# Two-bank tiles for the score maxima and for gate and up, three banks for everything else, in a two-layer transformer kernel

## The chip, the cores and the metric

The kernel runs on one core of a Trainium2 chip. The metric is the device time of one execution in microseconds (us), median of several runs. A core has a matrix engine (TensorE, PE in the profile, with its weight loads PEld), a vector engine (VectorE, DVE), an activation engine (ScalarE, ACT), GpSimd (POOL) and SyncE (SP), which issues DMAs. TensorE writes its results into PSUM, which this kernel divides into eight banks of 512 float32 elements in each of 128 partitions; VectorE and ScalarE read them from there.

## What is computed

Two transformer layers on x of 2 x 1024 x 256 float32 values. In each layer attention and a feed-forward network both start from the layer norm of x and are added to x. The change touches layer 0:

```python
xn = _layernorm(x, axis=-1)
x = x + _L0_attn_ref(xn, ...) + _L0_ffn_ref(xn, ...)

# _L0_attn_ref: 32 query heads, 8 key and value heads, 8 values a head, rope, causal
scores = jnp.einsum('bhqd,bhkd->bhqk', q, k_rep) / scale
scores = jnp.where((kpos > qpos)[None, None], -jnp.inf, scores)
attn = jax.nn.softmax(scores, axis=-1)
out = jnp.einsum('bhqk,bhkd->bhqd', attn, v_rep)
return out.transpose(0, 2, 1, 3).reshape(B, T, C) @ Wo + bo

# _L0_ffn_ref: 256 -> 1024 -> 256, operands rounded to e4m3, results in bfloat16
ff_gate = _qdot(x, w_gating[0])
gate_value = jax.nn.gelu(ff_gate)
ff1 = _qdot(x, w_gating[1])
outputs = _qdot(gate_value * ff1, w_linear)
```

Layer 1 has its own attention and a feed-forward network with ternary weights.

## The kernel before

Layer 0's attention (`attention0`) handles one block of 128 queries after another: `order` is the blocks (batch, i) of batch 0 rising and of batch 1 falling. A block i sees (i + 1) x 128 keys. Two passes are made over its scores.

The first finds the row maxima. A **unit** (`max_unit`) computes the scores of one, two or four pairs of heads into two banks, e = 0 and 1, which come from the two halves of the array's rows: `nc.tensor.matmul` at L843 for each e, the causal mask added by matmuls at L824 (`add_mask`). Then VectorE reduces each bank with its own `tensor_reduce` at L855. There are 304 units and 608 reductions. When a block's units are done, `take_max` (L869 to L873) splits the maxima into three bfloat16 parts, and `turn_max` transposes them and sends them through DRAM into the rows of the queries that subtract the maximum.

The second pass is made of 288 **weigh steps** (`weigh`). A step opens with two matmuls at L907 into two banks (e = 0, then e = 1), adds two more onto them, adds a mask (L824) on the diagonal, and ScalarE takes the exponential of each bank (L919). Every second step is preceded by a **gather** (L927): it multiplies the exponentials of two earlier steps with the values into the bank `acc`. Around it `normalise` (ot, L942), `turn_rows` (at, L958) and `output` (ao, L966) bring a finished group of heads out.

Between two weigh steps `one_slot` puts other work on TensorE: first one or several units of maxima of a later block, as a running credit of their cost allows, then a **piece** of the feed-forward network. In the pieces of `ffn0`, gate and up of 128 hidden columns for 512 tokens are two matmuls each (L284); ScalarE evicts each with a copy (L287), then GELU and rounding follow on ScalarE and VectorE in further pieces, and `out_piece` (f0o, L244) multiplies with the second weight. Other users of banks in this stage are the transposes of the layer norm (lnt, L178), the values (vp, L790), the maxima's transpose (mt, L878) and the group sums of layer 1's ternary weights (tps, L328).

TensorE's instructions run in the order in which the program makes them (`manual_schedule`). On the other engines the framework orders them, with `tc.issue_after(reduced.ins)` putting VectorE's share of a piece behind the last reduction made. A tile of a pool waits until a bank of that pool is free. The eight banks are divided so:

```python
ps_s = es.enter_context(tc.tile_pool(name="a0s", bufs=3, space=PSUM))
ps_t = es.enter_context(tc.tile_pool(name="a0t", bufs=4, space=PSUM))
ps_acc = es.enter_context(tc.tile_pool(name="a0acc", bufs=1, space=PSUM))
```

`ps_s` serves the maxima and the projections of queries and keys (`project`), one bank for each tile; `ps_t` serves weigh steps, gate and up, and all the other users named above.

Of the kernel before, what the change touches and what calls it, by code (L numbers as in the profile page):

```python
# [10 lines left out]
F32 = mybir.dt.float32  # L11
BF = mybir.dt.bfloat16
# [36 lines left out]
def two_layers(ctx: ExitStack, tc: tile.TileContext, a: dict, out: bass.AP):  # L49
# [179 lines left out]
                load(m)  # L229
            yield  # L230

    def ffn0(pool, psp, weights, add_done):

        wg, wl = weights
        acts = {}

        def e_tile(dt, name):
            t = pool.tile([P, 1024], F32, tag="fe", name=name, bufs=1)
            return t if dt == F32 else t.bitcast(BF)[:, 0:1024]

        def out_piece(n, i):
            po = psp.tile([P, D], F32, tag="t", name=f"f0o{n}_{i}")
            for hc in range(NHC):
                nc.tensor.matmul(  # L244
                    po,
                    acts[n][hc // 2][:, hc % 2 * 512 + i * P : hc % 2 * 512 + (i + 1) * P],
                    wl[:, hc, :],
                    start=(hc == 0),
                    stop=(hc == NHC - 1),
                )  # L250
            ob = pool.tile([P, D], BF, tag="ob", name=f"ob{n}_{i}", bufs=1)
            nc.scalar.copy(ob, po)  # L252
            x_i = xs[4 * n + i]
            nc.gpsimd.tensor_tensor(x_i, x_i, ob, ALU.add)
            nc.gpsimd.tensor_scalar(ob, ob, 0.0, None, ALU.mult)
            nc.gpsimd.tensor_tensor(x_i, x_i, ob, ALU.add)
            nc.gpsimd.tensor_tensor(x_i, x_i, bo_bc, ALU.add)
            add_done(4 * n + i)

        order = (0, 1, 3, 2)  # L260
        for m, n in enumerate(order):
            wide = pool.tile([P, 1024], F32, tag="fs", name=f"fsx{n}", bufs=1)
            xq = pool.tile([P, 2, 512], BF, tag="xq", name=f"xq{n}", bufs=1)
            yield from e4m3(
                xq.rearrange("p k t -> p (k t)"),
                xnT[n].rearrange("p k t -> p (k t)"),
                e_tile(F32, f"fex{n}"),
                wide,
                False,
            )  # L270
            yield
            acts[n] = []
            for h2 in range(NHC // 2):
                nm = f"{n}_{h2}"
                wide = pool.tile([P, 1024], F32, tag="fs", name=f"fs{nm}", bufs=1)
                w1, f1 = (wide.bitcast(BF)[:, k * 1024 : (k + 1) * 1024] for k in range(2))
                g = pool.tile([P, 1024], BF, tag="fg", name=f"fg{nm}", bufs=1)
                w2 = pool.tile([P, 1024], BF, tag="fw", name=f"fw{nm}", bufs=1)
                for j in range(2):
                    hc = 2 * h2 + j  # L280
                    for u, to in enumerate((g, f1)):
                        ps = psp.tile([P, 512], F32, tag="t", name=f"gu{nm}_{j}{u}")
                        for k in range(2):
                            nc.tensor.matmul(  # L284
                                ps, wg[:, u, k, hc * P : (hc + 1) * P], xq[:, k, :], start=(k == 0), stop=(k == 1)
                            )
                        nc.scalar.copy(to[:, j * 512 : (j + 1) * 512], ps)  # L287
                    yield

                nc.scalar.activation(w1, g, AF.Square)  # L290
                nc.vector.tensor_mul(w1, w1, g)
                nc.vector.tensor_scalar(w1, w1, GELU_C1, None, ALU.mult)
                yield
                nc.vector.tensor_add(w1, g, w1)
# [384 lines left out]
    def attention0(w, qlast, tables):  # L679
# [11 lines left out]
        with ExitStack() as es:  # L691
            pool = es.enter_context(tc.tile_pool(name="a0", bufs=2))
            es.enter_context(tc.manual_schedule(engines={mybir.EngineType.PE}))
            dram = es.enter_context(tc.tile_pool(name="a0d", bufs=2, space=bass.MemoryType.DRAM))
            ps_s = es.enter_context(tc.tile_pool(name="a0s", bufs=3, space=PSUM))
            ps_t = es.enter_context(tc.tile_pool(name="a0t", bufs=4, space=PSUM))
            ps_acc = es.enter_context(tc.tile_pool(name="a0acc", bufs=1, space=PSUM))
            units = ternary_units(pool, ps_t)
            kst, vst, qst, scratch = {}, {}, {}, {}
# [13 lines left out]

            def project(weights, lo, width, bias, b, c, name):

                ps = [ps_s.tile([P, 512], F32, tag="s", name=f"{name}p{e}") for e in range(2)]
                for e in range(2):
                    for k in range(2):
                        nc.tensor.matmul(
                            ps[e],  # L720
                            weights[:, k, e * width + lo : e * width + lo + P],
                            xnT[2 * b + c][:, k, :],
                            start=(k == 0),
                            stop=(k == 1),
                        )
                cs = slice(c * 512, (c + 1) * 512)
                y = []
                for e in range(2):
                    t = pool.tile([P, 512], F32, tag=f"y{e}", name=f"{name}y{e}", bufs=1)
                    nc.vector.scalar_tensor_tensor(t, ps[e], bias[:, e : e + 1], rope[:, e, cs], ALU.add, ALU.mult)  # L730
                    y.append(t)

                engine = nc.gpsimd if b or c else nc.vector
# [98 lines left out]
            def max_unit(b, i, pairs, lo, width, part, masked):  # L832
                if (b, i) not in mx:
                    mx[b, i] = pool.tile([P, 2, 2, NH0 // 2], F32, tag="mx", name=f"mx{b}{i}", bufs=3)
                n = len(pairs)
                sc = [ps_s.tile([P, 512], F32, tag="s", name=f"m{b}{i}_{pairs[0]}_{part}{e}") for e in range(2)]
                four = masked and width == P
                if four:
                    add_mask([x.rearrange("p (h k) -> p h k", h=4) for x in sc], mask_q, True, False)
# [11 lines left out]
                        end = (s + 1) * width  # L851
                        add_mask([x[:, end - P : end] for x in sc], mask_q, False, True)
                nonlocal reduced
                for e in range(2):
                    reduced = nc.vector.tensor_reduce(  # L855
                        mx[b, i][:, part, e, pairs[0] : pairs[0] + n],
                        sc[e][:, : n * width].rearrange("p (s k) -> p s k", s=n),
                        AX.X,
                        ALU.max,
                        negate=True,  # L860
                    )

            def take_max(b, i):
                both = mx.pop((b, i))
# [204 lines left out]

            acc = ps_acc.tile([P, 512], F32, tag="acc", name="acc0")  # L1070
            nc.vector.memset(acc, 0.0)
            pieces = itertools.chain(conversions, ffn0(pool, ps_t, weights, add_done))
            at = 0
            credit = share = 0.0
            cost_left = sum(cost for _, cost, _ in maxima)
# [169 lines left out]
```

## Time and profile before

| | |
|---|---|
| median of 3 runs | 1220.97 us (1217.82 to 1224.71) |
| the profiled execution | 1217.11 us, span 1215.3 us |
| mean granted TensorE clock | 0.903 |
| busy, of the span | PE 1044.4 us, DVE 738.2, ACT 572.8, PEld 501.8, POOL 265.4 |
| reductions of maxima (L855) | 608, busy 373.3 us |
| exponentials (L919) | 576, busy 307.5 us |
| first and last weigh step (L907) | 88.8 and 795.8 us |

The span is the time from the first to the last instruction. Busy time of an engine counts overlapping instructions once. A row of a group gives its line in the kernel, the engine, the operation, the tiles written and read, its count, busy us and mean ns of one, and the idle time of the engine just before it with what ended that. A row of the timeline gives start and duration in us, consecutive instructions of one kind merged (x2), and in brackets the idle time before it. Matmuls overlap, and the ends shown for them are modelled: an engine shown busy may still have been held.

### The profile page before, as it was taken

The numbers are of one execution on the slowest core, as the hardware profiler recorded it, in microseconds if no ns is written. First come the engines' busy times: TensorE is split into PE (matmuls) and PEld (weight loads), VectorE is DVE, ScalarE is ACT, GpSimd is POOL, SyncE is SP. The second block draws the span as 40 slices with busy tenths as digits, with TensorE's granted clock in tenths as the row PEclk, the third lists the DMA queues.
The fourth block names the chain that finished last, engine by engine and source line by source line (L and its number), as shares of the span: only waits on it lengthen the run. The fifth ranks groups of instructions, "written<-read, shape, count | busy, mean of one in ns | idle before, by whom it ended". The sixth has DMA issues, their size and how long they took to land.

```text
span 1215.3 us, 19246 instructions
## 1 busy us (share of the span) xinstructions
PE 1044.4 (86%) x7467; PEld 501.8 (41%) x7484; DVE 738.2 (61%) x1416; ACT 572.8 (47%) x990; POOL 265.4 (22%) x277
## 2 busy tenths in 40 slices
PE   6464897896988989898989998989999999998884
PEld 3233332232332223232323333335676676675673
DVE  7576988886867898788895889253223223323220
ACT  1113353662645757575767775741424414414421
POOL 3021022104053010501014115234313212312100
PEclk9576897997898989997999999999999999999785
DMA  6721001103011010100010110038211421411202
GB/s 193 168 80 37 22 15 38 26 2 90 1 26 27 2 26 18 35 1 18 10 27 3 25 26 5 3 30 120 54 28 45 75 40 45 77 39 28 44 11 53
DMA packets 79012, 49.01 MB, mean 40 GB/s; under 512 B 31720, under 2 KB 73704, under 8 KB 78920
## 3 DMA queue, kind: packets, MB, share of 16 engines
q1 hardware_dynamic: 75960, 43.58, 16.7%
q0 software_dynamic: 2960, 4.20, 1.7%
q8 instruction: 59, 0.97, 0.3%
q14 instruction: 33, 0.27, 0.1%
HBM read 33.59 MB, written 15.73 MB: 41 GB/s over the span
## 4 chain that ended last, share of the span: by engine, by line
PE 57%; DVE 21%; DMA 7%; issue 4%; ACT 4%; POOL 3%; SPq 2%; ACTq 0%; POOLq 0%; DVEq 0%
DVE mx L855 12%; PE acc L927 9%; PE s L907 8%; PE f1gu L610 7%; PE f1o L641 5%; PE m L843 4%; PE sk L520 3%; PE sq L485 3%; PE gu L284 2%; PE m L824 2%; PE s L824 2%; PE ao L586 2%; ACT p L528 2%; DMA qkv<-all 2%; PE acc L535 1%
## 5 line engine op out<-in xcount | busy, mean ns | idle before, releaser
L855 DVE TENSOR_REDUCE mx<-m 128x1 f32<-128x512 f32 (+3 forms) x608 | 373.3, 656 | 114.5 <-PE m L843 66.9
L919 ACT ACTIVATE p<-s 128x512 f32<-128x512 f32 x576 | 307.5, 603 | 163.5 <-PE s L907 115.3
L927 PE MATMUL acc<-p,v 128*9 128x512 f32 x1152 | 165.5, 626 | 0.0
L843 PE MATMUL m<-k,qmain 64*128 64x512 bf16 (+3 forms) x384 | 94.7, 368 | 44.3 <-DVE mx L855 28.4
L610 PE MATMUL f1gu<-xnT,wgu 128*128 128x512 f32 x256 | 118.9, 609 | 0.0
L843 PE MATMUL m<-kmain,qmain 64*128 64x512 bf16 (+3 forms) x384 | 82.4, 335 | 19.9 <-DVE mx L855 18.1
L824 PEld LDWEIGHTS <-ident_h 64*128 64x128 bf16 x1088 | 60.4, 97 | 92.3 <-issue 53.6
L843 PEld LDWEIGHTS <-qmain 64*128 64x128 bf16 x768 | 50.1, 100 | 89.0 <-issue 63.3
L824 PE MATMUL m<-mask_q,ident_h 64*128 64x128 bf16 (+1 forms) x832 | 82.0, 239 | 3.8 <-DVE mx L855 2.8
L618 DVE TENSOR_TENSOR h<-f1gu,h 128x512 f32<-128x512 f32 x32 | 22.1, 692 | 100.4 <-PE f1gu L610 97.0
L907 PE MATMUL s<-qlast,k 35*128 35x512 bf16 x288 | 66.3, 405 | 14.5 <-DMA qlast<-mscr 14.5
L907 PE MATMUL s<-qmain,k 64*128 64x512 bf16 x288 | 68.8, 409 | 11.3 <-ACT ob L252 5.8
L970 POOL TENSOR_TENSOR x<-x,aos 128x256 f32<-128x256 f32 x16 | 12.7, 792 | 300.5 <-ACT aos L969 300.5
L622 POOL TENSOR_TENSOR sq<-h 128x512 f32<-128x512 f32 x28 | 29.1, 1039 | 189.7 <-DVE h L618 189.7
L907 PEld LDWEIGHTS <-k 64*128 64x128 bf16 (+1 forms) x576 | 22.2, 97 | 114.5 <-issue 106.7
L610 PEld LDWEIGHTS f1gu<-xnT,wgu 128*128 128x128 f32 x256 | 48.1, 197 | 49.4 <-issue 49.3
L907 PE MATMUL s<-qmain,kmain 64*128 64x512 bf16 x288 | 64.2, 391 | 4.2 <-ACT p L919 2.4
L493 DVE TENSOR_REDUCE m<-sq 128x16 f32<-128x2048 f32 x16 | 36.7, 2292 | 44.8 <-PE sq L485 43.2
L907 PE MATMUL s<-qlast,klast 35*128 35x512 bf16 x288 | 61.2, 387 | 0.0
L641 PE MATMUL f1o<-k,h 128*128 128x256 f32 x256 | 58.9, 387 | 0.0
L641 PEld LDWEIGHTS f1o<-k,h 128*128 128x128 f32 x256 | 49.1, 194 | 8.2 <-issue 1.3
L907 PEld LDWEIGHTS <-kmain 64*128 64x128 bf16 x288 | 15.0, 94 | 78.1 <-issue 73.9
(267 smaller groups left out, 1588.1 us busy)
## 6 DMA issues: line engine op xcount, KB each, us to landing
qmain<-qscr SPq DMA_DIRECT2D x64, 96.0 KB
qkv<-all SPq DMA_DIRECT2D x16, 384.0 KB
qscr<-ptq SPq DMA_DIRECT2D x32, 96.0 KB
x<-in_x SPq DMA_DIRECT2D x16, 128.0 KB
qmain<-qscr SPq DMA_DIRECT2D x32, 64.0 KB
qs<-qkv SPq DMA_DIRECT2D x16, 128.0 KB
ks<-qkv SPq DMA_DIRECT2D x16, 128.0 KB
vs<-qkv SPq DMA_DIRECT2D x16, 128.0 KB
```

The lines of the kernel that those rows point to most:

```text
L485: nc.tensor.matmul(ps[:, s, r, :], columns(q, slice(S * s, S * s + HD + 8), 4 * b + r), columns(k, slice(S * s, S * s + HD + 8), 4 * b + r ...
L493: nc.vector.tensor_reduce(m, ps, AX.X, ALU.max, negate=True)
L520: nc.tensor.matmul(ps[:, s, r, :], columns(k, slice(S * s, S * s + HD + 9), 4 * b + r), columns(q, slice(S * s, S * s + HD + 9), 4 * b + r ...
L610: nc.tensor.matmul(ps[g], wgu[:, k, g * HID + hc * P : g * HID + (hc + 1) * P], xnT[n][:, k, :], start=(k == 0), stop=(k == 1),)
L622: nc.gpsimd.tensor_tensor(sq, h, h, ALU.mult)
L641: nc.tensor.matmul(po, hs[hc // 2][:, hc % 2, i * P : (i + 1) * P], wp[:, hc, :], start=(hc == 0), stop=(hc == NHC - 1),)
L824: nc.tensor.matmul(out[e], ident_h[rows, t, :], rhs, start=start and t == 0, stop=stop and t == 1)
L843: nc.tensor.matmul(sc[e][:, s * width : (s + 1) * width], qst[b, i][0][rows, p, :], kst[b][0][rows, p // 4, lo : lo + width], start=not fo ...
L855: reduced = nc.vector.tensor_reduce(mx[b, i][:, part, e, pairs[0] : pairs[0] + n], sc[e][:, : n * width].rearrange("p (s k) -> p s k", s=n ...
L907: nc.tensor.matmul(sc[e], kst[b][n][rows, u, j * P : (j + 1) * P], qst[b, i][n][rows, 4 * u : 4 * u + 4, :], start=n == 0, stop=n == 1 and ...
L919: nc.scalar.activation(p, sc[e], AF.Exp, scale=scale)
L927: nc.tensor.matmul(acc[32 * s : 32 * s + HD0 + 1, :], vst[b][:, j, 4 * G + s, :], ps[s], start=(j == 0), stop=(j == i),)
```

## The change

The maxima and the projections take one tile of two banks in place of two tiles of one bank; two such tiles make up the pool. One `tensor_reduce` reads both banks of a unit. Gate and up of one hidden chunk go into one two-bank tile of the same pool, and one copy evicts both; for that gate and up stand side by side in one buffer (`gf`), and `w1` moves to the buffer that held the gate. The pool for everything else has three banks in place of four.

```diff
-    def ffn0(pool, psp, weights, add_done):
+    def ffn0(pool, psp, ps_pair, weights, add_done):
...
-                w1, f1 = (wide.bitcast(BF)[:, k * 1024 : (k + 1) * 1024] for k in range(2))
-                g = pool.tile([P, 1024], BF, tag="fg", name=f"fg{nm}", bufs=1)
+                gf = wide.bitcast(BF).rearrange("p (u t) -> p u t", u=2)
+                w1 = pool.tile([P, 1024], BF, tag="fg", name=f"fg{nm}", bufs=1)
+                g, f1 = gf[:, 0], gf[:, 1]
...
-                    for u, to in enumerate((g, f1)):
-                        ps = psp.tile([P, 512], F32, tag="t", name=f"gu{nm}_{j}{u}")
+                    ps = ps_pair.tile([P, 2, 512], F32, tag="s", name=f"gu{nm}_{j}")
+                    for u in range(2):
                         for k in range(2):
                             nc.tensor.matmul(
-                                ps, wg[:, u, k, hc * P : (hc + 1) * P], xq[:, k, :], start=(k == 0), stop=(k == 1)
+                                ps[:, u],
+                                wg[:, u, k, hc * P : (hc + 1) * P],
+                                xq[:, k, :],
+                                start=(k == 0),
+                                stop=(k == 1),
                             )
-                        nc.scalar.copy(to[:, j * 512 : (j + 1) * 512], ps)
+                    nc.scalar.copy(gf[:, :, j * 512 : (j + 1) * 512], ps)
                     yield
...
-            ps_s = es.enter_context(tc.tile_pool(name="a0s", bufs=3, space=PSUM))
-            ps_t = es.enter_context(tc.tile_pool(name="a0t", bufs=4, space=PSUM))
+            ps_s = es.enter_context(tc.tile_pool(name="a0s", bufs=2, space=PSUM))
+            ps_t = es.enter_context(tc.tile_pool(name="a0t", bufs=3, space=PSUM))
...
-                ps = [ps_s.tile([P, 512], F32, tag="s", name=f"{name}p{e}") for e in range(2)]
+                ps = ps_s.tile([P, 2, 512], F32, tag="s", name=f"{name}p")
...
-                sc = [ps_s.tile([P, 512], F32, tag="s", name=f"m{b}{i}_{pairs[0]}_{part}{e}") for e in range(2)]
+                pair = ps_s.tile([P, 2, 512], F32, tag="s", name=f"m{b}{i}_{pairs[0]}_{part}")
+                sc = [pair[:, e] for e in range(2)]
...
-                for e in range(2):
-                    reduced = nc.vector.tensor_reduce(
-                        mx[b, i][:, part, e, pairs[0] : pairs[0] + n],
-                        sc[e][:, : n * width].rearrange("p (s k) -> p s k", s=n),
-                        AX.X,
-                        ALU.max,
-                        negate=True,
-                    )
+                reduced = nc.vector.tensor_reduce(
+                    mx[b, i][:, part, :, pairs[0] : pairs[0] + n],
+                    pair[:, :, : n * width].rearrange("p e (s k) -> p e s k", s=n),
+                    AX.X,
+                    ALU.max,
+                    negate=True,
+                )
...
-            pieces = itertools.chain(conversions, ffn0(pool, ps_t, weights, add_done))
+            pieces = itertools.chain(conversions, ffn0(pool, ps_t, ps_s, weights, add_done))
```

More of the change, by code (lines that the diff above doesn't have):

```diff
@@ L719, in project @@
                         nc.tensor.matmul(
-                            ps[e],
+                            ps[:, e],
                             weights[:, k, e * width + lo : e * width + lo + P],
@@ L729, in project @@
                     t = pool.tile([P, 512], F32, tag=f"y{e}", name=f"{name}y{e}", bufs=1)
-                    nc.vector.scalar_tensor_tensor(t, ps[e], bias[:, e : e + 1], rope[:, e, cs], ALU.add, ALU.mult)
+                    nc.vector.scalar_tensor_tensor(t, ps[:, e], bias[:, e : e + 1], rope[:, e, cs], ALU.add, ALU.mult)
                     y.append(t)
```

## The prediction

> **What bounds the kernel now.** I read the busy time by windows first, then the chain of waits, the groups kept apart by shape, the list of waits, and last the timeline, row by row.
>
> ```profile
> PE 57%; DVE 21%; DMA 7%; issue 4%; ACT 4%; POOL 3%; SPq 2%; ACTq 0%; POOLq 0%; DVEq 0%
> ...
> 700.00:750.00 50.00, 47.14 (x457) 19.44 (x456) 43.63 (x95) 33.52 (x65) 14.28 (x14) 1.00 0.09 18
> ...
> L855 DVE TENSOR_REDUCE mx<-m 128x1 f32<-128x512 f32 x384 | 245.8, 684 | 68.4 <-PE m L843 47.3 <-PE m L824 20.9
> L855 DVE TENSOR_REDUCE mx<-m 128x1 f32<-128x384 f32 x128 | 65.7, 551 | 21.7 <-PE m L824 20.9
> L493 DVE TENSOR_REDUCE m<-sq 128x16 f32<-128x2048 f32 x16 | 36.7, 2292 | 44.8 <-PE sq L485 43.2 <-DMA out<-x 1.5
> ...
> PE m L843 <- DVE mx L855: 46.5, 84, 1.9
> ```
>
> Layer 0's attention lasts from 88.8 us, where the first weigh step begins, to 797. In a window there (us busy of 50: PE, PEld, DVE, ACT, POOL) no engine is full: PE has 47, DVE 44, ACT 34. PE runs a written order, so any wait in it is lost. The only large entry in the wait list that holds PE there is L843, the maxima's matmuls, waiting for the reduction at L855. The timeline shows how:
>
> ```profile
> 412.96 0.39 PE L907 MATMUL s<-qmain,k 64*128 64x512 bf16 x2
> 413.18 0.38 PE L907 MATMUL s<-qlast,k 35*128 35x512 bf16 x2
> 413.40 0.38 PE L843 MATMUL m<-k,qmain 64*128 64x512 bf16 x2
> 413.62 0.27 PE L824 MATMUL m<-mask_q,ident_h 64*128 64x128 bf16 x4
> 413.73 0.38 PE L907 MATMUL s<-qmain,k 64*128 64x512 bf16 x2
> 413.95 0.38 PE L907 MATMUL s<-qlast,k 35*128 35x512 bf16 x2
> 414.17 0.38 PE L843 MATMUL m<-k,qmain 64*128 64x512 bf16 x1
> 414.94 0.37 PE L843 MATMUL m<-k,qmain 64*128 64x512 bf16 x1 [0.40 <-DVE mx L855]
> 414.95 0.48 PE L824 MATMUL m<-mask_q,ident_h 64*128 64x128 bf16 x4
> 415.36 1.04 PE L927 MATMUL acc<-p,v 128*9 128x512 f32 x8
> ...
> 413.66 2.06 ACT L919 ACTIVATE p<-s 128x512 f32<-128x512 f32 x4 [0.74 <-PE s L907]
> 414.21 2.50 DVE L855 TENSOR_REDUCE mx<-m 128x1 f32<-128x512 f32 x4
> ```
>
> The columns are start, duration, engine, line. A weigh step (L907) opens at 412.96, a unit of maxima follows, a second step at 413.73, a second unit, a gather (L927). The two matmuls of a unit normally start 3 ns apart. At 414.17 and 414.94 they are 0.77 apart: with three single banks the second needs the bank that the previous unit's first reduction holds. The reported idle time (0.40) is less than the loss, since the first matmul is still shown running.
>
> So I measured the loss as the distance of the two starts, over all 384 pairs of L843: **102.4 us in 196 pairs** beyond 10 ns each. Of it 53.0 lies in 265 ordinary intervals from one weigh step to the next (at most two pairs of matmuls), 37.5 in 22 intervals with more (bursts), and 11.9 before 88.8 us.
>
> [...] 684 - 551 ns over 128 elements is 1.04 ns each, which leaves 151 ns fixed. [...] The change moves banks from one rotation to another.
>
> **The reduction.** 608 instructions become 304 of double width. L493 already reads four banks at 2292 ns, so two should take 1024 x 1.04 + 151 = 1.22 us. In runs back to back, records overlap: 2.50 us for four is 0.62 each, hence about 1.15 per double one. DVE saves 0.085 to 0.15 per pair, 26 to 46 us in all, of which only what holds PE counts. The first half can no longer start alone, but its two matmuls end nearly together, so I add nothing; if they don't, each unit is up to 0.2 later.
>
> **The maxima's banks.** With two pairs, a unit waits for the unit before last as a whole. That is at least one single reduction (0.6 us) earlier than now, so in ordinary intervals I let these waits go. In bursts DVE itself has no room (15 reductions in the 12.0 us from 428.4 to 440.4, DVE busy 93%); there only its saving counts. 126 reductions lie in bursts: 63 x 0.085 = 5.4 us, up to all 37.5 where DVE is not full. I take -9. Before 88.8 us the path goes through loads and POOL, DVE is 66% busy: -2, from 0 to -12.
>
> **Three banks for the rest.** This is the cost. A weigh step needs two banks, freed by the exponentials (L919) of the step before. With four banks it finds two free. With three, its second opening matmul must wait for the first exponential of the step before, and everything on PE behind it waits too. In the lines above: the step of 412.96 has its exponentials from 413.66, the first frees its bank at 413.66 + 0.60 (a single one), plus 0.05 until PE goes on, 414.31. The next step wants it at 413.73: **0.58 us late**. A step after a gather comes 1 us later and finds it free.
>
> I did this for every step: the end of the exponential plus 0.05, less the start of the matmul; with all other tiles of that pool (ot, at, ao, mt, tps, f0o, lnt, vp) in the rotation and gate/up taken out of it. The same rule with four banks, gate/up included, accounts to within 70 ns for 42 of the 58 steps whose second matmul is already late now, so I trust it. With three it makes 124 of 287 steps wait, 75.6 us. 110 of them are among the 144 steps that no gather precedes (65.2 us), 14 among the 143 others (10.4).
>
> These waits and the ones removed partly replace each other, so I went through the intervals in PE's order: subtract each distance removed, and where a bank is later than the shifted matmul, set the shift to it. In ordinary intervals this gives 83.8 us of lengthening and 44.4 of shortening: **+39.4**. Two things take from that. Twenty-three gathers already wait for exponentials now (10.5 us more than the usual length), as the last steps show:
>
> ```profile
> 776.21 2.07 ACT L919 ACTIVATE p<-s 128x512 f32<-128x512 f32 x4 [1.17 <-PE s L824]
> ...
> 776.48 1.89 PE L927 MATMUL acc<-p,v 128*9 128x512 f32 x8
> ```
>
> The gather takes 1.89 us where 1.04 is usual; a step that is late ahead of it only uses up this wait: -10 (0 to -10.5). And the exponentials of a late step are queued on ACT behind the earlier ones anyway, so the steps after gathers wait less than listed: half of 10.4, -5 (0 to -10).
>
> **Gate and up.** 32 evictions of 1024 elements replace 64 of 512 (609 and 593 ns). ACT's rows give 603 ns for 512 and 1877 for 2048, so 0.83 ns an element and 1.03 us for 1024: 0.17 x 32 = 5.4 us less of ACT, which is idle a third of the time there; I count 0 (0 to -5). Without that cover it would be the whole 5.4. In the maxima's rotation, gate and up now wait for the reduction of the unit before last: 18 of the 32 come earlier than that today, 5.1 us, and units behind them or behind one another 2.1. I take +4 (0 to +7). The exchange of w1 and g between two buffers leaves the instructions as they are; the buffer of f1 comes free earlier, that of the other is first written later: 0, within 1 us either way. No DMA and no step is moved, so SP's and POOL's queues keep their order; POOL waits for DVE in long idle stretches and gets nothing tighter.
>
> **Sum.** 39.4 - 10 - 5 - 9 - 2 + 4 = +17.4 us. The profiled execution took 1217.1 us (span 1215.3 and 1.8 around it); the median of the three runs is 3.9 above. So 1234.5 against the profile, and **1238** as a median. Layer 1, from about 800 us, is untouched and moves as a whole.
>
> **Rivals.**
> *Faster: ACT gives its bank back soon enough.* What speaks for it: 102 us of waits on DVE are at stake, and the rule applied to today's times ignores that a delayed PE meets a less loaded ACT. If bursts yield 20 and the early part 6, then 44.4 + 26 goes, and new waits of 40 come: -30, 1191. The deciding point: the waits at steps not behind a gather. The sum is zero when the whole of new waits, 69 net in my account, is 51, or 0.35 us for each of the 144 steps instead of 0.48. Against it: the 0.58 is a latency from PE to ACT and back, shown with ACT idle before it (0.74 in the row), which no slack shortens.
> *An even swap:* bursts yield 25 instead of 9: about +1, 1222.
> *Much slower:* a fixed rotation makes a step wait for the second exponential, 0.49 us later, where another bank is free. In a third of the 110 steps that is +18, with no help from the gathers +28 more at most: up to 1280. Against it: the few misfits of my rule with four banks.
> *The wide reduction isn't cheaper* (two banks at 2 x 684): the gain of bursts and of the early part goes, +11, 1249. L493 speaks against it.
>
> **How the numbers follow.** A measurement of this kernel can tell some 0.5% from no change, 6.1 us. My case 0.45, much slower and not cheaper 0.13 together, even swap 0.16, faster 0.26. The range reaches from half way into the faster rival to half way into the much slower one, 1206 to 1270. The unknown terms of my own case reach about as far. With bursts and early part at their best (-38.5) it is 1200. With all at their worst (gathers +10, steps after gathers +5, gate and up +3, bursts +3.6, early part +2) and the late half costing 0.1 us in each of 304 units (+30) it is 1292, and half way there 1265.
>
> **What would show it.** Reductions: 304, near 1.2 us each. The two matmuls of a unit start together outside bursts, and L843's waits on L855 fall from 46.5 us below 20. The second matmul of L907 starts late, some 0.5 us, in about 110 steps, most of them not behind a gather; PE's waits on L919 rise from 4.1 us to tens. Gate/up evictions: 32, near 1.03 us. Ordinary steps about 0.1 us longer, layer 1 as long as before. I am wrong if L907's pairs start together, if L843 still waits as much, or if the last weigh step ends before 795 us.

## The result, and the profile after

| | before | after |
|---|---|---|
| median (6 runs each) | 1217.33 us | 1229.42 us |
| lowest to highest | 1212.75 to 1224.71 | 1225.93 to 1230.88 |
| span of the profiled execution | 1215.3 us | 1229.1 us |
| first weigh step opens | 88.8 us | 85.5 us |
| last weigh step opens | 795.8 us | 808.9 us |

The changed kernel is slower: ratio 1.0085, 95% interval 1.0061 to 1.0108. The changed kernel's lines are numbered a little higher: the steps are L912, the maxima's matmuls L849, the reduction L860, the exponential L924. Its page sums the chain of waits so:

```profile
PE 56%; DVE 17%; ACT 10%; issue 5%; DMA 5%; POOL 4%; SPq 1%; ACTq 0%; POOLq 0%; DVEq 0%
```

The window from 700 to 750 us of the changed kernel (window and length, then busy us and count of PE, PEld, DVE, ACT and POOL, then the granted clock, the DMA's share and GB/s):

```profile
700.00:750.00 50.00, 44.06 (x421) 18.08 (x419) 39.22 (x64) 34.33 (x62) 11.38 (x10) 1.00 0.09 18
```

Its groups by shape (busy us and mean ns of one, then idle time ahead):

```profile
L860 DVE TENSOR_REDUCE mx<-m 128x2 f32<-128x1024 f32 x192 | 231.9, 1220 | 86.3 <-PE m L849 56.3 <-PE m L829 29.3
L860 DVE TENSOR_REDUCE mx<-m 128x2 f32<-128x768 f32 x64 | 60.1, 953 | 25.3 <-PE m L829 25.3
L292 ACT CAST fs<-gu 128x1024 bf16<-128x1024 f32 x32 | 32.4, 1012 | 37.3 <-PE gu L285 37.2
```

And its list of waits (sum in us, count, longest in us):

```profile
PE m L849 <- DVE mx L860: 33.7, 40, 2.3
PE s L912 <- ACT p L924: 31.4, 67, 3.2
```

The last of these rows read so in the kernel before:

```profile
PE s L907 <- ACT p L919: 4.1, 7, 1.5
```

Each new instruction takes what its rows foretold: 1220 ns for a reduction of two banks, 1012 ns for the eviction of gate and up. But in the chain DVE's share falls from 21 to 17% while ACT's rises from 4 to 10%, and PE is less busy in the same window, 44.06 us for 47.14. The steps' wait for ACT grew from 4.1 to 31.4 us. The timeline shows it in the cycle of two steps, two units and a gather, the same that the prediction took apart:

```profile
407.31 0.39 PE L912 MATMUL s<-qmain,k 64*128 64x512 bf16 x2
407.53 0.38 PE L912 MATMUL s<-qlast,k 35*128 35x512 bf16 x2
407.75 0.38 PE L849 MATMUL m<-k,qmain 64*128 64x512 bf16 x2
407.97 0.27 PE L829 MATMUL m<-mask_q,ident_h 64*128 64x128 bf16 x4
408.08 0.38 PE L912 MATMUL s<-qmain,k 64*128 64x512 bf16 x1
408.65 0.37 PE L912 MATMUL s<-qmain,k 64*128 64x512 bf16 x1 [0.20 <-ACT p L924]
408.66 0.58 PE L912 MATMUL s<-qlast,k 35*128 35x512 bf16 x2
408.89 0.58 PE L849 MATMUL m<-k,qmain 64*128 64x512 bf16 x2
409.11 0.47 PE L829 MATMUL m<-mask_q,ident_h 64*128 64x128 bf16 x4
409.51 1.04 PE L932 MATMUL acc<-p,v 128*9 128x512 f32 x8
410.48 0.39 PE L912 MATMUL s<-qmain,k 64*128 64x512 bf16 x2
```

The second unit's two matmuls (408.89) no longer wait for VectorE. Instead the second step's opening pair is torn apart, 408.08 and 408.65: 0.57 us, where 0.58 was foretold. The reported idle time is again smaller (0.20), because the first matmul is still shown running (0.38 us from 408.08). The torn opening also leaves a lag of 0.20 us between the two matmuls of the unit behind it, with no wait in their row. One wait has taken the place of the other: this cycle lasts 3.17 us where it took 3.38 before, and the next one 3.18 for 3.11.

The loss lies elsewhere. An interval is the time from one weigh step's opening to the next; an ordinary one has at most two pairs of the units' matmuls in it, a burst more. Call a pair torn when its two matmuls start over 50 ns apart. The 96 ordinary intervals in which a unit had been torn before come out 14.5 us shorter in sum, and the other 169 come out 36.6 us longer.

Counted over the whole trace as in the prediction, the distances between the starts of the two matmuls, where beyond 10 ns, are:

| us | before | after |
|---|---|---|
| two matmuls of a unit (L843, now L849) | 102.4 | 26.5 |
| two opening matmuls of a step (L907, now L912) | 30.3 | 72.7 |
| steps late by over 50 ns, without / with a gather ahead | 55 / 3 | 111 / 10 |

Of the 26.5 us, 22.6 lie behind torn openings and are for the most part the lag just described. These distances are a sign of where PE was held and no account of the time: their sum falls from 132.7 to 99.2 us, while the kernel gets slower.

Where the 13.8 us between the two profiled spans lie, interval by interval between the openings of the same steps: ordinary intervals +22.1 (66.3 longer, 44.2 shorter), bursts -5.7, up to the first step -3.3, after the last +0.6.

### The profile page after: what moved, and what is told of

The parts are those of the page before. It is cut to its first block, busy times and chain, and to the rows that moved or that the text cites. A ratio compares the mean times of both kernels' runs of the same rounds, so it can differ in the third digit from the quotient of the medians.

```text
span 1229.1 us, 18929 instructions
## 1 busy us (share of the span) xinstructions
PE 1029.4 (84%) x7484; PEld 503.0 (41%) x7484; DVE 720.1 (59%) x1112; ACT 579.6 (47%) x958; POOL 266.3 (22%) x277
## 4 chain that ended last, share of the span: by engine, by line
PE 56%; DVE 17%; ACT 10%; issue 5%; DMA 5%; POOL 4%; SPq 1%; ACTq 0%; POOLq 0%; DVEq 0%
DVE mx L860 9%; PE s L912 9%; PE f1gu L615 8%; PE acc L932 8%; PE f1o L646 5%; ACT p L924 4%; PE sk L525 3%; PE sq L490 3%; PE gu L285 3%; PE m L849 2%; PE s L829 2%; ACT p L533 2%; PE m L829 2%; PE acc L540 1%; PE ao L591 1%
## 5 line engine op out<-in xcount | busy, mean ns | idle before, releaser
L860 DVE TENSOR_REDUCE mx<-m 128x2 f32<-128x1024 f32 (+3 forms) x304 | 350.4, 1164 | 139.6 <-PE m L849 76.4
L924 ACT ACTIVATE p<-s 128x512 f32<-128x512 f32 x576 | 313.0, 595 | 174.0 <-PE s L912 117.0
L849 PE MATMUL m<-k,qmain 64*128 64x512 bf16 (+3 forms) x384 | 74.1, 370 | 34.3 <-DVE mx L860 25.4
L912 PE MATMUL s<-qmain,k 64*128 64x512 bf16 x288 | 77.8, 407 | 25.2 <-ACT p L924 15.1
L912 PE MATMUL s<-qmain,kmain 64*128 64x512 bf16 x288 | 78.2, 386 | 19.2 <-ACT p L924 16.3
L849 PEld LDWEIGHTS <-qmain 64*128 64x128 bf16 x768 | 53.0, 100 | 98.8 <-issue 71.8
L829 PEld LDWEIGHTS <-ident_h 64*128 64x128 bf16 x1088 | 67.4, 98 | 44.6 <-issue 5.4
L912 PE MATMUL s<-qlast,k 35*128 35x512 bf16 x288 | 70.5, 405 | 12.1 <-DMA qlast<-mscr 12.1
L849 PE MATMUL m<-kmain,qmain 64*128 64x512 bf16 (+3 forms) x384 | 72.4, 338 | 9.4 <-DVE mx L860 8.3
L623 DVE TENSOR_TENSOR h<-f1gu,h 128x512 f32<-128x512 f32 x32 | 22.1, 692 | 98.9 <-PE f1gu L615 98.9
L912 PEld LDWEIGHTS <-k 64*128 64x128 bf16 (+1 forms) x576 | 23.5, 96 | 134.6 <-issue 124.5
L829 PE MATMUL m<-mask_q,ident_h 64*128 64x128 bf16 (+1 forms) x832 | 77.2, 240 | 0.0
L912 PE MATMUL s<-qlast,klast 35*128 35x512 bf16 x288 | 69.0, 384 | 0.0
L292 ACT CAST fs<-gu 128x1024 bf16<-128x1024 f32 x32 | 32.4, 1012 | 37.3 <-PE gu L285 37.2
```

The lines of the kernel that those rows point to most:

```text
L829: nc.tensor.matmul(out[e], ident_h[rows, t, :], rhs, start=start and t == 0, stop=stop and t == 1)
L849: nc.tensor.matmul(sc[e][:, s * width : (s + 1) * width], qst[b, i][0][rows, p, :], kst[b][0][rows, p // 4, lo : lo + width], start=not fo ...
L860: reduced = nc.vector.tensor_reduce(mx[b, i][:, part, :, pairs[0] : pairs[0] + n], pair[:, :, : n * width].rearrange("p e (s k) -> p e s k ...
L912: nc.tensor.matmul(sc[e], kst[b][n][rows, u, j * P : (j + 1) * P], qst[b, i][n][rows, 4 * u : 4 * u + 4, :], start=n == 0, stop=n == 1 and ...
L924: nc.scalar.activation(p, sc[e], AF.Exp, scale=scale)
```

## The experiments

The theory: the loss is the steps' wait for a bank, since the pool of steps has three in place of four; what the maxima gain by their fourth bank doesn't pay for it. Rival one: the two-bank tile costs (its reduction starts late and both banks come free together). Rival two: gate and up cost, through their place in the maxima's pool or through the single copy. A third, left for later, was that the waits only cover a bound elsewhere.

In each run the ratio is to the kernel before on the same chip; between runs on different chips the ratios are the fairer comparison. Distances are those of the table above, units first, then steps. Where both matmuls of a unit wait together for a two-bank tile, the wait is plain idle time and no distance (d_one_pair_five: 142.0 us of idle time at L849, 5.0 us of distances).

| run | banks: maxima + rest | median us | ratio (95%) | units | steps |
|---|---|---|---|---|---|
| before | 3 + 4 | 1216.6 to 1219.0 | 1 | 102.4 | 30.3 |
| after | two pairs + 3 | 1229.42 | 1.0085 (1.0061 to 1.0108) | 26.5 | 72.7 |
| a_three_only | 3 + 3 | 1246.87 | 1.0250 (1.0221 to 1.0279) | 95.9 | 66.6 |
| b_four_singles | 4 + 3 | 1225.05 | 1.0071 (1.0046 to 1.0096) | 57.5 | 68.2 |
| c_gu_in_three | two pairs + 3 | 1224.67 | 1.0072 (1.0046 to 1.0097) | 28.7 | 74.7 |
| d_one_pair_five | one pair + 5 | 1277.05 | 1.0512 (1.0477 to 1.0546) | 5.0 | 2.9 |
| k_four_three | 4 + 3 | 1225.41 | 1.0068 (1.0045 to 1.0092) | 59.1 | 69.9 |
| n_two_copies | two pairs + 3 | 1232.29 | 1.0109 (1.0090 to 1.0129) | 26.1 | 72.9 |
| g_after_order | two pairs + 3 | 1229.54 | 1.0084 (1.0051 to 1.0117) | 7.7 | 50.6 |
| h_before_order | 3 + 4 | 1259.20 | 1.0342 (1.0309 to 1.0375) | 146.6 | 17.4 |
| j_four_three_order | 4 + 3 | 1218.51 | 1.0000 (0.9983 to 1.0018) | 43.7 | 52.9 |
| l_shared_seven | 7 shared | 1178.42 | 0.9667 (0.9644 to 0.9689) | 51.0 | 19.8 |
| m_shared_order | 7 shared | 1184.36 | 0.9718 (0.9699 to 0.9737) | 41.7 | 27.6 |
| o_shared_six | 6 shared | 1203.13 | 0.9877 (0.9855 to 0.9899) | 61.3 | 30.2 |

**The third bank alone (a_three_only).** The kernel before, with

```diff
-            ps_t = es.enter_context(tc.tile_pool(name="a0t", bufs=4, space=PSUM))
+            ps_t = es.enter_context(tc.tile_pool(name="a0t", bufs=3, space=PSUM))
```

> The kernel before with one edit: the pool of the weigh steps and of everything else has three banks instead of four; the maxima keep three single banks, gate and up stay in the pool of three, one bank is unused. Theory 'third bank' (the loss of the change is the steps' wait for the first exponential of the step before): the second opening matmul of L907 starts late in over 110 steps, 70 us or more in sum beyond 10 ns (30.3 before). Part of that covers the maxima's waits for VectorE, which stay (L843's distance falls from 102 to 60 to 80 us), so the time is 20 to 45 us over before: 1237 to 1262, slower than the changed kernel. Theory 'two-bank tiles' (a unit starts late and both banks come free together) and theory 'gate and up' (they hold up the maxima's rotation): both say that the fourth bank was spare, within 5 us of before.

Measured: 1246.87, some 30 us over before. The rivals, which called the fourth bank spare, are out as the main cause. The steps' distances are 66.6 (70 expected). The units' remain 95.9, where 60 to 80 was expected. The timeline of this run shows where the two kinds of waits cover each other and where they don't:

```profile
420.09 0.39 PE L907 MATMUL s<-qmain,k 64*128 64x512 bf16 x2
...
420.86 0.38 PE L907 MATMUL s<-qmain,k 64*128 64x512 bf16 x1
421.44 0.37 PE L907 MATMUL s<-qmain,k 64*128 64x512 bf16 x1 [0.20 <-ACT p L919]
421.44 0.58 PE L907 MATMUL s<-qlast,k 35*128 35x512 bf16 x2
421.67 0.58 PE L843 MATMUL m<-k,qmain 64*128 64x512 bf16 x2
...
423.26 0.39 PE L907 MATMUL s<-qmain,k 64*128 64x512 bf16 x2
```

The step waits 0.58 us for its bank, and meanwhile VectorE finishes, so the unit behind it (421.67) waits for nothing: 3.17 us again. Such cycles lose nothing by the third bank; the others do.

**Four single banks (b_four_singles).** The division of the changed kernel, without a two-bank tile: `ps_s` with four banks, `ps_t` with three, gate and up as single tiles of `ps_s`, two reductions and two copies.

```diff
-            ps_s = es.enter_context(tc.tile_pool(name="a0s", bufs=3, space=PSUM))
-            ps_t = es.enter_context(tc.tile_pool(name="a0t", bufs=4, space=PSUM))
+            ps_s = es.enter_context(tc.tile_pool(name="a0s", bufs=4, space=PSUM))
+            ps_t = es.enter_context(tc.tile_pool(name="a0t", bufs=3, space=PSUM))
...
-                        ps = psp.tile([P, 512], F32, tag="t", name=f"gu{nm}_{j}{u}")
+                        ps = ps_pair.tile([P, 512], F32, tag="s", name=f"gu{nm}_{j}{u}")
```

> The banks divided as in the changed kernel (four for maxima and gate/up, three for the rest), but as four single banks: two reductions for each unit, two evictions for gate and up. Theory 'third bank': as the changed kernel, with VectorE's 26 us of saving undone and bursts 5 us longer: 1230 to 1240, L843's distances small (under 40 us), L907's as in the changed kernel (60 to 80 us). Theory 'two-bank tiles': back to 1213 to 1221. Theory 'gate and up' (rotation): as the changed kernel within 4 us.

Measured: 1225.05, below the 1230 to 1240 expected and above the 1221 of rival one. The units' distances are 57.5, where under 40 was expected, and yet the time is no longer than with two-bank tiles. So the loss comes with the division of banks and needs no two-bank tile; the double reduction's saving on VectorE did not show in the time.

**Gate and up back (c_gu_in_three).** The changed kernel with

```diff
-                    ps = ps_pair.tile([P, 2, 512], F32, tag="s", name=f"gu{nm}_{j}")
                     for u in range(2):
+                        ps = psp.tile([P, 512], F32, tag="t", name=f"gu{nm}_{j}{u}")
...
-                    nc.scalar.copy(gf[:, :, j * 512 : (j + 1) * 512], ps)
+                        nc.scalar.copy(gf[:, u, j * 512 : (j + 1) * 512], ps)
```

> The changed kernel with gate and up back in the pool of the weigh steps, two single banks and two copies; that pool still has three banks. Theory 'third bank': more users of the three banks, L907's distances rise by 5 to 20 us, the maxima lose 8 us of waits behind gate and up: 1229 to 1241. Theory 'gate and up': the loss goes, 1222 or less. Theory 'two-bank tiles': unchanged within 4 us of the changed kernel.

Measured: 1224.67, less than the theory's 1229, more than rival two's 1222. Against 1229.42 it is 4.7 us by the medians and 3.8 by the profiled spans, but the ratios, 1.0072 and 1.0085, have intervals that overlap, so the runs do not tell the two apart. The steps' distances rose only from 72.7 to 74.7, where 5 to 20 more was expected: gate and up are no burden on the three banks.

**Two copies (n_two_copies).** The changed kernel, the tile kept and only the single copy undone:

```diff
-                    nc.scalar.copy(gf[:, :, j * 512 : (j + 1) * 512], ps)
+                    for u in range(2):
+                        nc.scalar.copy(gf[:, u, j * 512 : (j + 1) * 512], ps[:, u])
```

> The changed kernel with two copies of 512 for gate and up in place of one of 1024, the two-bank tile kept in the maxima's pool. Taking gate and up out of that pool gave 4.7 us. If that was the rotation (a pair of banks held, the maxima's turn delayed), nothing comes back: 1227 to 1233, the pair being released 0.17 us later. If it was the single copy, which waits for both halves and keeps ACT from exponentials for 1.0 us at a stretch, it is 1222 to 1226.

Measured: 1232.29. Nothing comes back, so the single copy is not what gate and up cost. What they do cost would then lie in the rotation. The trace points there: in the changed kernel PE stands idle 7.7 us ahead of their matmuls for the reduction, in the run with gate and up in the three banks 0.2.

```profile
PE gu L285 <- DVE mx L860: 7.7, 10, 1.1
```

The size of this cost, some 4 us, is not shown beyond the noise.

**One pair and five (d_one_pair_five).** The opposite division: c_gu_in_three with `ps_s` at one pair and `ps_t` at five banks.

> The opposite division: the maxima have one pair of banks, the rest (gate and up with it) five. Theory 'third bank': L907's distances nearly vanish (under 15 us, 30.3 before), and every unit now waits until VectorE has done with the one before, so PE waits for the reduction far more than the 49.7 us before at L843: over 120 us; the time is 40 to 90 us over before, 1257 to 1307. If the steps' banks didn't matter, L907's distances would be as in the kernel before and the time higher still.

Measured: 1277.05. From its list of waits:

```profile
PE m L849 <- DVE mx L860: 142.0, 132, 4.9
```

PE's wait for the reduction is 142.0 us, for 46.5 in the kernel before, and the steps' distances are 2.9. The units' distances nearly vanish too, but only because both matmuls of a unit now wait together. So both pools are short, and each bank given to one is taken from the other.

**The division alone (k_four_three).** The kernel before with nothing but `bufs` changed to four and three.

> The kernel before with nothing but the banks moved: four single banks for maxima, three for the rest, gate and up in the three, two reductions and two evictions. Theory 'third bank', with what the runs so far gave (the four single banks with gate and up among them 1225.1; gate and up out of the maxima's banks 4 us less): 1219 to 1226, L907's distances 65 to 80 us. If the two-bank tiles or the single eviction mattered to the loss, it is at the time before, 1217 or less.

Measured: 1225.41, +6.4 us on the median of its own chip, within the expected band. The changed kernel is 12.1 us over its own; by the ratios it is 0.68 of 0.85%. So the division alone brings half of the loss or more. Two-bank reductions on top (c_gu_in_three, 1.0072) make no difference that can be told. Neither does it matter whether gate and up take their single banks among the maxima's four (b_four_singles, 1.0071) or among the three (1.0068). The rest may come from gate and up as a pair; that is not shown beyond the noise.

**Another order of the units (g_after_order, h_before_order, j_four_three_order).** The steps that wait are those with little ahead of them (in the changed kernel 111 of the 121 late ones have no gather ahead). In these runs units of maxima are placed only there, twice as many:

```diff
-            def one_slot(weights):
+            def one_slot(weights, u=0):
...
-                credit = min(credit + rate, 2.0 * rate)
-                while at < len(maxima) and credit > 0 and order[maxima[at][0]] in qst:
-                    advance()
+                if u == 0:
+                    if weights:
+                        rate *= 2.0
+                    credit = min(credit + rate, 2.0 * rate)
+                    while at < len(maxima) and credit > 0 and order[maxima[at][0]] in qst:
+                        advance()
...
-                            one_slot(True)
+                            one_slot(True, u)
```

g_after_order is the changed kernel so:

> The changed kernel with one edit in TensorE's order: units of maxima are placed only ahead of the steps that no gather precedes (twice as many there), none where the gather stands. Theory 'third bank': the steps that waited get one more unit of matmuls (0.33 to 0.65 us) ahead of them, so the exponential of the step before is nearly done: L907's distances fall from 72.7 to 20 to 45 us, and 15 to 35 us come off the changed kernel, 1195 to 1215; it may then be ahead of the kernel before. If the steps' waits only covered a bound elsewhere (ACT or VectorE), the distances fall and the time stays at 1225 to 1233.

h_before_order is the kernel before so:

> The same order of the units in the kernel before, with its division of three single banks for maxima and four for the rest. Theory 'third bank': its steps seldom wait, so there is little to gain there, and two units back to back wait more for the three banks of the maxima: L843's distances rise from 102 to 110 to 150 us; 1217 to 1240. If the order itself is the gain, it is as much faster than before as the other kernel is faster than the changed one (15 us or more, below 1203).

j_four_three_order is k_four_three so:

> Four single banks for maxima, three for the rest, gate and up in the three, single reductions, and the order of units as in the two kernels above (only ahead of steps that no gather precedes). Theory 'third bank': both kinds of waits are small, L843's distances under 60 and L907's 20 to 45 us; 1190 to 1212, the fastest of these four or level with the changed kernel in this order.

Measured: 1229.54, 1259.20 and 1218.51, all three outside what was expected. The middle one went the theory's way and further: two units in a row find three banks too few, the units' distances rise to 146.6, and it costs 40 us, where 23 at most was expected. The last gains 6.9 us on k_four_three and only reaches the time before, not 1212; its steps' distances are 52.9, over the 45 expected. The first is the plainest miss. The steps' distances fell by 22 us and the units' by 19, and the time didn't move. That is the outcome which the expectation gave to a bound elsewhere, and the shared pool below has to answer it. The timeline shows the wished-for cycle, and beside it new waits:

```profile
400.09 0.27 PE L829 MATMUL m<-mask_q,ident_h 64*128 64x128 bf16 x4
401.12 0.39 PE L912 MATMUL s<-qmain,k 64*128 64x512 bf16 x1 [0.76 <-DVE att L955]
402.49 0.37 PE L912 MATMUL s<-qmain,k 64*128 64x512 bf16 x1 [0.98 <-ACT p L924]
...
408.20 0.39 PE L912 MATMUL s<-qmain,k 64*128 64x512 bf16 x2
...
408.65 0.38 PE L849 MATMUL m<-k,qmain 64*128 64x512 bf16 x2
...
408.98 0.38 PE L849 MATMUL m<-k,qmain 64*128 64x512 bf16 x2
...
409.31 0.62 PE L912 MATMUL s<-qmain,k 64*128 64x512 bf16 x2
...
411.05 0.39 PE L912 MATMUL s<-qmain,k 64*128 64x512 bf16 x2
```

From 408.20 on, two units stand together, the step behind them (409.31) opens as a pair, and the cycle takes 2.85 us. But a step at 401.12 waits 0.76 us for VectorE to read the transposed outputs (att) out of one of the three banks. PE's wait ahead of gate and up for the reduction grew from 7.7 to 14.5 us. Such waits took part of the gain; where all of it went wasn't followed up.

**One pool (l_shared_seven).** The theory says that a bank of the wrong pool is free while PE waits. This run is the kernel before with both pools made one:

```diff
-            ps_s = es.enter_context(tc.tile_pool(name="a0s", bufs=3, space=PSUM))
-            ps_t = es.enter_context(tc.tile_pool(name="a0t", bufs=4, space=PSUM))
+            ps_s = ps_t = es.enter_context(tc.tile_pool(name="a0t", bufs=7, space=PSUM))
...
-                ps = [ps_s.tile([P, 512], F32, tag="s", name=f"{name}p{e}") for e in range(2)]
+                ps = [ps_s.tile([P, 512], F32, tag="t", name=f"{name}p{e}") for e in range(2)]
...
-                sc = [ps_s.tile([P, 512], F32, tag="s", name=f"m{b}{i}_{pairs[0]}_{part}{e}") for e in range(2)]
+                sc = [ps_s.tile([P, 512], F32, tag="t", name=f"m{b}{i}_{pairs[0]}_{part}{e}") for e in range(2)]
```

> The kernel before with one pool of seven single banks for maxima, steps and all else, in place of three and four; instructions and TensorE's order unchanged. Theory 'third bank' (both kinds of waits are for a bank of the right pool, while the other pool has one free): in the cycle of two steps, two units and a gather, six banks are held before the second unit, so most of both waits go. L907's distances under 25 us, L843's under 50 (102.4 before); 15 to 45 us under before, 1172 to 1204. If the bound is ACT's or VectorE's work and the waits only show it, or if the framework's choice of banks binds them as firmly as two pools do, the time is within 6 us of before.

Measured: 1178.42, 40 us under before and 51 under the changed kernel, with the same instructions in the same order on PE. Its list of waits (steps L906, units L842, exponentials L918, reductions L854):

```profile
PE m L842 <- DVE mx L854: 14.9, 30, 1.7
...
PE s L906 <- ACT p L918: 8.0, 5, 6.5
```

And one cycle of its timeline:

```profile
395.70 0.39 PE L906 MATMUL s<-qmain,k 64*128 64x512 bf16 x2
...
396.14 0.38 PE L842 MATMUL m<-k,qmain 64*128 64x512 bf16 x2
...
396.47 0.38 PE L906 MATMUL s<-qmain,k 64*128 64x512 bf16 x2
...
396.91 0.51 PE L842 MATMUL m<-k,qmain 64*128 64x512 bf16 x2
397.12 0.41 PE L823 MATMUL m<-mask_q,ident_h 64*128 64x128 bf16 x4
397.46 1.10 PE L926 MATMUL acc<-p,v 128*9 128x512 f32 x8
398.50 0.39 PE L906 MATMUL s<-qmain,k 64*128 64x512 bf16 x2
```

No matmul of the cycle waits (the second unit's two start 0.14 us apart), and it takes 2.80 us; the same two steps took 3.11 before and 3.18 in the changed kernel. Most of the gain is not in such cycles, though. Of the 36.4 us between the profiled spans, 22.1 lie in bursts, where the maxima can now take more than three banks, 9.2 in ordinary intervals and 5.8 ahead of the first step.

This run also ends the rival that ACT or VectorE bounds the stage by its work: the work is the same, and the last weigh step opens at 758.7 us in place of 795.8. For the other order of the units m_shared_order below shows the same against h_before_order.

**One pool, other order and fewer banks (m_shared_order, o_shared_six).** The shared pool with the order above, and the shared pool with `bufs=6`.

> One pool of seven single banks, and units of maxima only ahead of steps that no gather precedes. Two units in a row hold four banks, and the step after them wants two more while two are still held by the step before: L843's distances above those of the pool of seven without this order (50 to 100 us), L907's under 35. Theory 'third bank': slower than the shared pool alone by 5 to 30 us, but ahead of this order with three and four banks (1259.2) by over 20. If the order is good in itself, it is ahead of the shared pool.

> The shared pool with six banks in place of seven, one bank unused: as many banks as three and three, which took 1246.9. Theory 'third bank', in the form that the waits come from dividing the banks: six shared ones still serve better than three and three, 1190 to 1225, with L907's and L843's distances between those of the shared seven (19.8 and 51.0 us) and those of three and three (66.6 and 95.9). If the shared pool gained by the number of banks that a step can use and not by sharing, six fall back to 1235 or more.

Measured: 1184.36, 5.9 us slower than the shared pool alone, at the lower edge of what was expected; the order is no gain in itself. The units' distances went the other way than expected, from 51.0 down to 41.7. Six shared banks give 1203.13, and three and three, as many, 1246.87. So it is the sharing. Fixed divisions other than those of the table were not tried.

## Why the prediction came out as it did

By its own steps, in us, the prediction against the profiled execution before:

| step | foretold | measured |
|---|---|---|
| lengthening of ordinary intervals, net of gathers and steps behind them | 68.8 | 66.3 |
| shortening of ordinary intervals | -44.4 | -44.2 |
| gate and up in the maxima's pool | +4 | within the two above (+4.7 by the medians against c_gu_in_three, not beyond noise) |
| bursts | -9 | -5.7 |
| before the first step | -2 | -3.3 |
| after the last | 0 | +0.6 |
| sum | +17.4 | +13.8 |

**The wait that was foretold is there.** 110 steps without a gather ahead were to wait 65.2 us; 111 did, by 63.8. The wait in the cycle was 0.57 for 0.58. Of the 121 late steps of the trace after, 80 go on 0.05 us after the end of the first exponential of the step before, as the rule has it, and 24 as long after the end of the second. The rule, worked on the trace before without the pool's other tiles, names 101 steps late by over 50 ns; 91 of them are late after. That the waits on VectorE would go in ordinary intervals was right too.

**That the sum came so near is in part luck.** 55 of the 111 steps were late before, by 25.8 of the 63.8 us. Here is what became later or earlier in the 265 ordinary intervals, by the instruction of PE ahead of which the time was gained or lost (the distance from the start of the one before it, after less before):

| ahead of | us |
|---|---|
| the second opening matmul of a step and the two added onto the pair | +35.9 |
| matmuls and masks of units | -35.2 |
| the first opening matmul of a step | +15.1 |
| the maxima's transpose, group sums, f0o, gate and up | +15.8 |
| gathers and values | -9.4 |
| sum, with -0.1 of others | +22.1 |

So the exchange that the prediction worked out, late second openings for freed units, came out even, where its terms gave +24 (39.4 - 10 - 5). The growth lies in claims that it put at nothing: the first opening matmul of a step, and of the row below it the transpose of the maxima (6.6), the group sums (5.0) and f0o (2.7). In the 125 ordinary intervals where neither an opening nor a unit was torn in either trace, the sum is +22.5 us. The first opening's loss comes with the three banks: it is 14.7 to 16.4 us in a_three_only, b_four_singles, c_gu_in_three and k_four_three, and 2.1 in l_shared_seven. The maxima's transpose (+6.6) is another matter, since it waits for VectorE's splitting of the maxima (by the lists of waits 12.6 us after, 5.4 before, 15.7 in l_shared_seven), and it is as late in l_shared_seven (+7.1); why stays open.

Two smaller terms were off as well. The absorption by gathers was set to -10, but the gathers' own excess fell only from 10.5 to 6.8 us. The 14 late steps behind gathers were priced at 10.4 us and halved to 5; 10 were late, by 9.0.

**The distance is not the loss.** The prediction took the distance of two starts as what a torn pair costs. In the cycle that it shows, 0.77 us of distance make 3.38 us, where l_shared_seven, with 0.14, takes 2.80: 0.58 are lost. In the changed kernel the torn opening of the same two steps, 0.57, costs 0.38 by the same comparison. Both times the distance is too large by about 0.2 us and the idle time too small by as much.

**The rest of the distance to 1238** is in the base. I added the 3.9 us by which three runs' median exceeded the profiled execution; six runs brought the median before down to 1217.33. The profiled execution after is on the other side of its median (1230.9 against 1229.4). The forecast growth of 17.4 stands against 12.1 by the medians.

**Mis-sized: the double reduction.** I priced its gain in bursts at 0.085 us a pair, from 2.50 us for four single ones. But these 2.50 us are three distances of starts and one whole reduction of 0.68, so one comes every 0.60 us and not every 0.62. Back to back the double one starts every 1.134 us, against 2 x 0.601 before, so 0.068, and over the kernel DVE's busy time at the line falls by 22.9 us, under the foretold 26 to 46. More to the point, the gain in bursts was not its own. With four single banks and single reductions (k_four_three) bursts shorten by 17.8 us, with two pairs by 5.7 to 7.7. The pairs get back about as much in ordinary intervals (20.0 longer in c_gu_in_three against 28.9). And three banks with single reductions (a_three_only) shorten bursts by 9.1 us too, though nothing of the maxima's was changed there. So the step "bursts" had the right sign, but the wide instruction is not needed for it, and neither is the fourth bank. Why bursts shorten, and why four single banks do best, stays open.

**Missed: the sign to look for at L843.** Its waits for the reduction were to fall below 20 us and stand at 33.7. In ordinary intervals they did fall, from 19.4 to 5.4. In bursts and before the first step they are 28.3 after 27.1. There both matmuls of a unit now wait for the pair, so what had lain hidden behind a running matmul shows as idle time (the distances there fell from 49.4 to 6.3 us).

**The rivals of the prediction.** The faster one needed new waits of 51 us or less. All lengthening of ordinary intervals is 66, but the steps' distances alone grew by no more than 42.4; without the 22.5 us of the untorn intervals the change would by this account (an estimate: 13.8 - 22.5) have gained some 9 us. So that rival failed through the claims which nobody had priced. The much slower one, a step held to the second exponential, would have put the cycle at 1.07 us of wait; it is at 0.57. It holds for 24 of the 121 late steps; that another bank was free then is not shown. By its own terms the upper end of that rival is 1284 (1238 + 18 + 28), not 1280. The wide reduction is cheaper per element (1220 ns for 1024 against 684 ns for 512), and its price was not what mattered.

## What to carry to other kernels

Before dividing PSUM anew, take the lifetime of each bank in one cycle of TensorE's order, from the first matmul into it to the end of its reader. Then count how many a pool needs at the moment of each claim, of the small users too: a claim that comes one bank short waits until the reader of the bank is done, here 0.57 us in the cycle shown and 0.52 in the median of 121 late steps. Where two users claim at different moments of the cycle, one pool for both can serve better than a fixed division, here better than every one that was tried: seven banks shared took 1178.4 us, where three and four took 1219 and four and three 1225.

## What was not expected

- A wide instruction's saving on an engine that isn't full can be worth nothing: 22.9 us less of VectorE's busy time, and c_gu_in_three (1224.67) stands level with k_four_three (1225.41).
- A torn pair doesn't show in the wait list at its size. When the second of two matmuls on separate halves of the array waits, the first is still shown as running: the list before has 46.5 us at L843, where the distances sum to 102.4. In the cycles compared the loss lay about midway between the two.
- Waits in one cycle can cover each other. Taking one of four banks away cost 30 us (a_three_only), with 66.6 us of distances at the steps against 30.3; giving that bank to the maxima brought back 21.5 of the 30 (k_four_three).
